# A conditioned two-layer feed-forward kernel: layer 1's adapters computed for four chunks in one go, in four PSUM banks

## The chip, the cores and the metric

The kernel runs on one core of one Trainium2 chip. The metric is the device time of one execution in microseconds (us), as the median of several runs; lower is better. Everything is float32. In the trace the engines are called PE (TensorE, the matrix engine; its weight loads are a row of their own, PEld), DVE (VectorE), ACT (ScalarE), POOL (GpSimd) and SP (SyncE, which here only issues DMAs).

## The reference, cut to what matters

The input `x` has 64 batches x 32 positions x 512 features, that is 2048 tokens. Layer 0 (a long convolution, then a linear layer with routed low-rank adapters) is added to `x`; layer 1 follows. The change touches only the first half of layer 1, a gated feed-forward block of width F = 1376 in which every batch has a low-rank adapter of rank 16 of its own:

```
def lora_add(base, inp, A, B):
    Ab = A[layer_idx][lora_indices]
    Bb = B[layer_idx][lora_indices]
    t = jnp.einsum('bri,bni->bnr', Ab, inp)
    return base + jnp.einsum('bor,bnr->bno', Bb, t) * SCALE
gate = lora_add(jnp.einsum('bnh,fh->bnf', x, W_gate), x, A_gate, B_gate)
up = lora_add(jnp.einsum('bnh,fh->bnf', x, W_up), x, A_up, B_up)
act = jax.nn.silu(gate) * up
down = lora_add(jnp.einsum('bnf,hf->bnh', act, W_down), act, A_down, B_down)
```

Its result goes to a mixture of 16 experts, whose router first computes `logits = x2 @ gate_w.T` of the layer's input and takes the two best experts for each token.

## The kernel before, in words

**Order of the work.** The instructions of PE, DVE and ACT run in exactly the order in which the Python code names them (`tc.manual_schedule` over these three engines); waits between engines are put in by the framework. So "earlier in the code" means earlier in that engine's queue, and an instruction that waits holds up all that stand behind it on its engine. The DMAs that SP and POOL issue are placed by the framework.

**Groups and chunks.** Layer 1's gated block works through 8 groups of 8 batches (`for g in range(NG)`), a group being 256 tokens, and in each group through 11 chunks of 128 of the 1376 (padded to 1408) hidden features (`for j in range(NF)`). In one chunk:

- PE forms gate and up of the chunk as seven products of half-size blocks (a Strassen-like scheme, `by_blocks`, L789): four of them into one PSUM bank `gu`, three into a second bank `gum` (`more` in the code). Both come from the pool `ps_mm`, which has two banks; they take turns, so `gu` of chunk j has the bank of `gu` of chunk j-1 as long as nothing else takes one.
- ACT copies `gu` to SBUF (L925). DVE adds the parts up (L928, L929, L930), adds the adapter's share (L931), and then adds what is in `gum` (L937, L938). L938 is the last reader of the bank `gum`.
- ACT takes the Silu (L940), DVE multiplies (L942), and PE multiplies the result by `W_down` one chunk later (`down`, L852), adding up in the four banks `zp` of the pool `ps_acc`.

**The adapters.** `adapted` (L791) computes the adapters' share of gate and up. The adapter of a group is a product over 64 rows, so two matmuls of 64 rows run side by side in the upper and lower half of PE's array (L802, `which` 0 and 1), each into its own bank. In the kernel before, it is called at every even j for two chunks, takes the two banks of the pool `ps_td`, and ACT copies both to the SBUF tile `los` (L807). I call the L802 matmuls of one call a **visit**: PE comes from the 128-row products, does a visit and goes back. There are six visits in a group, at j = 0, 2, 4, 6, 8 (two chunks) and 10 (one chunk). In the trace each matmul of this float32 code counts as two, so a visit for two chunks shows as x16.

**What else uses the same banks and queues.**

- At the end of a group: `ranks` (L825, the adapters' first factor for the next group; DVE copies it out in L835), the last `down`, then `own` (L866 to L876): DVE reads `zp` four times (L866), and ACT and DVE each copy two halves of it to `zt` (L876).
- In chunk j = 0 of the next group: `turn_own` (PE L880, ACT L882) between the two banks of the chunk, and `adapt` (PE L889, DVE L892) at its end; in j = 1 `turn` (PE L901, four transposes per bank, two banks of `ps_td`, copied out by DVE and ACT in L904).
- In groups 2, 4 and 6 the router's logits: at the end of j = 2 `logits` (PE L735, ACT L737), at the end of j = 3 `by_tokens` (PE L743 turns them, DVE L745 copies them out; one bank of `ps_td`), and in j = 4 and 5 `chosen` (softmax and the two best, about twenty small DVE operations and an Exp on ACT).
- At j = 6 `gathered_down` (four ACT copies, L454) for the next group's adapters, which POOL gathers by indirect DMA in j = 2 to 8 (L432); small DVE copies `columns` (L445) from j = 6 on. In group 0 DVE also forms sums of weights in each chunk up to j = 8 (`combine`, L209 to L212, four operations).

Of the kernel before, what the change touches and what calls it, by code (L numbers as in the profile page):

```python
# [9 lines left out]
F32 = mybir.dt.float32  # L10
I32 = mybir.dt.int32
AF = mybir.ActivationFunctionType
ALU = mybir.AluOpType
# [4 lines left out]
P = 128  # L18
# [8 lines left out]
F, NF = 1376, 11  # L27
# [10 lines left out]
NG, TG = B // GB, GB * H  # L38
# [4 lines left out]
FP = NF * P  # L43
# [60 lines left out]
def kernel(ctx: ExitStack, tc: tile.TileContext, a: dict, out: bass.AP):  # L104
    nc = tc.nc
    mm, tt, ts = nc.tensor.matmul, nc.vector.tensor_tensor, nc.vector.tensor_scalar
# [6 lines left out]
    ps_mm = ctx.enter_context(tc.tile_pool(name="ps_mm", bufs=2, space=PSUM))  # L113
    ps_td = ctx.enter_context(tc.tile_pool(name="ps_td", bufs=2, space=PSUM))
    ps_acc = ctx.enter_context(tc.tile_pool(name="ps_acc", bufs=4, space=PSUM))

    def bank(pool, name):
        return pool.tile([P, TB], F32, tag="bank", name=name)
# [5 lines left out]
    def rows(x, n):  # L124

        return x.unsqueeze(1).to_broadcast([x.shape[0], n, x.shape[1]])
# [47 lines left out]
    first = ExitStack()  # L174
# [18 lines left out]
    def fetch(n):  # L193

        g, j = divmod(n, NF)
        blocks[n] = stream.tile([P, 7 * BW], F32, tag="w", name=f"w_{n}")
        if g == 0:
            nc.sync.dma_start(blocks[n][:, 0 : 4 * BW], a["cw"][j])
        else:
            nc.sync.dma_start(blocks[n][:, 0 : 3 * BW], a["cw"][j][:, 0 : 3 * BW])  # L200
            nc.sync.dma_start(blocks[n][:, 3 * BW :], sums_d[j])
# [4 lines left out]
    def combine(n):  # L206

        a11, a12, a22, a21, s2, s3, s4 = (block(n, i) for i in range(7))
        tt(s3, a11, a21, ALU.subtract)  # L209
        tt(a21, a21, a22, ALU.add)  # L210
        tt(s2, a21, a11, ALU.subtract)
        tt(s4, a12, s2, ALU.subtract)  # L212
        (nc.gpsimd if n < 2 else nc.sync).dma_start(sums_d[n], blocks[n][:, 3 * BW :])
# [9 lines left out]
    def small(n=H):  # L223
        part = next(r for r in room if r[1] >= n)
        part[1] -= n
        return part[0][:, part[1] : part[1] + n]
# [46 lines left out]
    start = small(1)  # L273
# [187 lines left out]
    with tc.tile_pool(name="l0", bufs=1) as l0, tc.tile_pool(name="l0b", bufs=2) as l0b:  # L461
# [48 lines left out]
        def by_tokens(tb, yT):  # L510

            for i in range(4):
                n = tb * 4 + i
                gt = bank(ps_td, f"gt_{n}")
                for c in range(NC):
                    mm(
                        gt[:, 0 : G0 + P],
                        yT[:, c, i * P : (i + 1) * P],
                        ag[:, c, :],
                        start=(c == 0),  # L520
                        stop=(c == NC - 1),
                    )
                tt(hg[:, n, :], gt[:, 0:G0], row0[:, 0:G0], ALU.add)
                nc.scalar.copy(tmp[tb][:, i, :], gt[:, G0 : G0 + P])
# [261 lines left out]
    def by_blocks(to, n, i, x):  # L786

        for c in range(2):
            mm(to, block(n, i)[:, c * P : (c + 1) * P], x[:, c], start=(c == 0), stop=(c == 1))  # L789

    def adapted(g, j, r, wb):  # L791


        js = range(j, min(j + 2, NF))
        banks = [bank(ps_td, f"lo_{g}_{j}_{which}") for which in range(2)]
        for k, half in ((k, half) for k in js for half in (1, 0)):
            at = (k - j) * TG + (1 - half) * P
            lo = half * FP + k * P
            for which in range(2):
                mine = slice(which * P // 2, (which + 1) * P // 2)  # L800
                to = banks[which][:, at : at + P]
                mm(to, wb[mine, lo : lo + P], r[mine, half, :], start=True, stop=True)  # L802
        to = l1.tile([P, 2, 4, P], F32, tag="lo", name=f"los_{g}_{j}", bufs=1)
        n = len(js)
        for which in range(2):
            src = banks[which][:, 0 : n * TG].rearrange("p (j k t) -> p j k t", j=n, k=2)
            nc.scalar.copy(to[:, 0:n, 2 * which : 2 * which + 2], src)  # L807
        return to

    l1s = ExitStack()  # L810
    l1 = l1s.enter_context(tc.tile_pool(name="l1c", bufs=2))
# [8 lines left out]
    def ranks(g, wr):  # L820

        ps = bank(ps_td, f"r_{g}")
        for half in range(2):
            for c in range(NC):
                mm(  # L825
                    ps[:, half * P : (half + 1) * P],
                    wr[:, half, c, :],
                    batches(g, c, half),
                    start=(c == 0),
                    stop=(c == NC - 1),  # L830
                )
        r = l1.tile([P, 2, P], F32, tag="r", name=f"rs_{g}")
        own = cst[:, C_HALF : C_HALF + HG].unsqueeze(1).to_broadcast([P, 2 * H, HG])
        by_batch = ps[:, 0 : 2 * P].rearrange("p (n b) -> p n b", b=HG)
        tt(r.rearrange("p k (h b) -> p (k h) b", b=HG), by_batch, own, ALU.mult)  # L835
        return r
# [71 lines left out]
    r = ranks(0, wr)  # L908
    differ(0)
    past = None  # L910
    for g in range(NG):
        wa, wb, wd = got[g]
        this = Group(g)
        before = None
        for j in range(NF):
            n = g * NF + j
            (b11, b12, b21, b22), (t1, t2, t3, t4) = halves[g], differences[g]
            if j % 2 == 0:
                adapters = adapted(g, j, r, wb)
            ps = bank(ps_mm, f"gu_{g}_{j}")  # L920
            for at, i, x in ((0, 4, t2), (1, 0, b11), (2, 5, t3), (3, 2, t4)):
                by_blocks(ps[:, at * P : (at + 1) * P], n, i, x)
            gu = l1.tile([P, 4, P], F32, tag="gu", name=f"gus_{g}_{j}")
            flat = gu.rearrange("p k t -> p (k t)")
            nc.scalar.copy(flat, ps)  # L925
            if j == 0 and past is not None:
                past.turn_own()
            tt(gu[:, 0], gu[:, 0], gu[:, 1], ALU.add)  # L928
            tt(gu[:, 2], gu[:, 2], gu[:, 0], ALU.add)  # L929
            tt(gu[:, 3], gu[:, 3], gu[:, 2], ALU.add)  # L930
            tt(flat, flat, adapters[:, j % 2].rearrange("p k t -> p (k t)"), ALU.add)  # L931
            more = bank(ps_mm, f"gum_{g}_{j}")
            for at, i, x in ((0, 6, b22), (1, 1, b21), (2, 3, t1)):
                by_blocks(more[:, at * P : (at + 1) * P], n, i, x)
            if n + 4 < NG * NF:
                fetch(n + 4)
            tt(flat[:, 0:TG], flat[:, 0:TG], more[:, 0:TG], ALU.add)  # L937
            tt(gu[:, 0:3:2], gu[:, 0:3:2], rows(more[:, TG : TG + P], 2), ALU.add)  # L938
            si = glu.tile([P, TB], F32, tag="si", name=f"si_{g}_{j}")[:, 0:TG]
            nc.scalar.activation(si, flat[:, 0:TG], AF.Silu)  # L940
            at = glu.tile([P, TB], F32, tag="at", name=f"at_{g}_{j}")[:, 0:TG]
            tt(at, si, flat[:, TG:], ALU.mult)  # L942
            at = at.rearrange("p (k t) -> p k t", k=2)
            if g == 0 and j + 2 < NF:
                combine(j + 2)
            if g + 1 < NG and j == 9:
                differ(g + 1)
            if past is not None:
                if j == 0:
                    past.adapt()  # L950
                if j == 1:
                    past.turn()
                    columns(g, 9)
                if j == 2:
                    columns(g, 10)
            if g + 1 < NG and j >= 2:
                if j == 2:
                    coming.append(Adapters(g + 1))
                    got.append(coming[-1].all())
                coming[-1].rows(2 if j < 6 else 1)  # L960
            if before is not None:
                this.down(j - 1, before)
            before = at
            if g % 2 == 0 and g > 0:
                if j == 2:
                    lt = logits(g // 2 - 1)
                if j == 3:
                    by_tokens(g // 2 - 1, lt)
                if j == 4:
                    choice = chosen(g // 2 - 1)  # L970
                    next(choice)
                if j == 5:
                    run(choice)
            if g + 1 < NG and 6 <= j:
                if j == 6:
                    wr = gathered_down(g + 1)
                for i in ((0, 1), (2, 3), (4, 5), (6, 7), (8,))[j - 6]:
                    columns(g + 1, i)
        if g + 1 < NG:
            r = ranks(g + 1, wr)  # L980
            this.down(NF - 1, before)
            this.own()
        past = this


# [424 lines left out]
```

## Time and profile before

| | |
|---|---|
| median of 3 runs | 1040.71 us (1040.18 to 1041.33) |
| the profiled execution, its own time | 1042.03 us |
| its span, first to last instruction | 1040.2 us |
| PE busy | 1009.4 us (97%) |
| DVE, ACT, POOL busy | 563.7, 254.1, 168.4 us |
| granted TensorE clock | 1.000 of full speed over the whole span |
| the chunk loop of layer 1, first visit to last `down` of group 7 | 167.9 to 719.8 us |

In a timeline row the first number is the start in us from the beginning of the span, the second the time from the start of the first to the end of the last instruction of the merged row, then the engine, the line in the kernel, the operation, written tile <- read tiles, the shape, and the count; in brackets stands how long the engine sat idle before it and what released it. PE's matmuls overlap, so the time that a step takes is read from start to start, not from the durations. In a row of the waits stand: who waited, on which line, for whom; the total in us, how many times, and the longest.

### The profile page before, as it was taken

How to read it: one execution, taken by the hardware profiler on the slowest of the kernel's cores; microseconds unless marked ns; L12 is line 12 of the kernel's file. 1: busy time of each engine (PE TensorE's matmuls, PEld its weight loads, DVE VectorE, ACT ScalarE, POOL GpSimd, SP SyncE). 2: the span in 40 equal slices, each digit the busy share in tenths (PEclk: the TensorE clock that was granted, in tenths of full speed). 3: DMA queues.
4: the chain of work that ended last, by engine and by line, in shares of the span. 5: the costliest groups of instructions: out<-in, count | busy, mean ns of one | idle time of the engine just before them, and what ended most of it. 6: DMA issues, size and time to landing. Idle time of an engine off the chain costs nothing. (4 is left out here: it accounts for less than half of the span.)

```text
span 1040.2 us, 16572 instructions
## 1 busy us (share of the span) xinstructions
PE 1009.4 (97%) x6112; PEld 767.4 (74%) x6112; DVE 563.7 (54%) x1772; ACT 254.1 (24%) x509; POOL 168.4 (16%) x188
## 2 busy tenths in 40 slices
PE   3999999999999999999999999999999999999998
PEld 2777657888888888888888888897445677775453
DVE  5656566775464755656655556544632333332562
ACT  2222012222322332324223233232100222221000
POOL 2131001210201202102012021000000332221720
PEclk9999999999999999999999999999999999999999
DMA  6656409784755746646567457431930455555651
GB/s 179 203 210 225 134 20 344 242 286 147 237 180 185 243 155 205 232 160 210 184 197 248 147 194 242 147 123 38 418 132 11 121 163 164 169 168 178 203 183 60
DMA packets 63824, 189.42 MB, mean 182 GB/s; under 512 B 8448, under 2 KB 11552, under 8 KB 63104
## 3 DMA queue, kind: packets, MB, share of 16 engines
q1 hardware_dynamic: 49072, 137.52, 38.0%
q0 software_dynamic: 14096, 50.76, 16.3%
q8 instruction: 51, 0.84, 0.3%
q14 instruction: 29, 0.24, 0.1%
q10 hardware_dynamic: 576, 0.07, 0.1%
HBM read 157.56 MB, written 30.75 MB: 181 GB/s over the span
## 5 line engine op out<-in xcount | busy, mean ns | idle before, releaser
L852 PE MATMUL zp<-wn,at 128*128 128x288 f32 x704 | 185.4, 406 | 0.8 <-DVE at L942 0.8
L789 PE MATMUL gu<-t,w 128*128 128x128 f32 x1056 | 152.5, 281 | 0.0
L852 PEld LDWEIGHTS zp<-wn,at 128*128 128x128 f32 x704 | 127.1, 190 | 28.9 <-DVE at L942 0.9
L789 PEld LDWEIGHTS gu<-t,w 128*128 128x128 f32 x1056 | 133.9, 191 | 14.8 <-issue 5.9
L770 PE MATMUL sgu<-xall,sw 128*128 128x512 f32 (+2 forms) x272 | 114.1, 570 | 0.0
L432 POOL DMA_INDIRECT wa<-in_la,row_a x64 | 61.3, 958 | 309.8 <-issue 108.5
L928 DVE TENSOR_TENSOR gus<-gus 128x128 f32<-128x128 f32 x88 | 25.7, 292 | 134.6 <-ACT gus L925 134.6
L940 ACT ACTIVATE si<-gus 128x256 f32<-128x256 f32 x88 | 36.7, 417 | 244.7 <-DVE gus L938 244.7
L789 PE MATMUL gum<-xall,w 128*128 128x128 f32 x704 | 93.2, 275 | 0.8 <-DVE gus L938 0.7
L770 PEld LDWEIGHTS sgu<-xall,sw 128*128 128x128 f32 x272 | 49.7, 190 | 55.1 <-issue 53.5
L789 PEld LDWEIGHTS gum<-xall,w 128*128 128x128 f32 x704 | 85.7, 192 | 1.2 <-PE gu L789 1.1
L1186 POOL DMA_INDIRECT zr<-zd,tok x42 | 39.5, 941 | 255.3 <-DVE tok L1163 160.5
L1205 PE MATMUL egu<-wall,zx 128*128 x336 | 80.5, 382 | 0.0
L1205 PEld LDWEIGHTS egu<-wall,zx 128*128 128x128 f32 x336 | 60.5, 189 | 19.5 <-ACT zx L1196 12.5
L925 ACT COPY gus<-gu 128x512 f32<-128x512 f32 x88 | 51.4, 584 | 78.5 <-PE gu L789 78.5
L802 PEld LDWEIGHTS lo<-rs,wb 64*128 64x128 f32 x704 | 45.9, 187 | 26.2 <-issue 14.2
L802 PE MATMUL lo<-rs,wb 64*128 64x128 f32 x704 | 57.0, 287 | 5.8 <-ACT xall L904 2.5
L931 DVE TENSOR_TENSOR gus<-gus,los 128x512 f32<-128x512 f32 x88 | 60.9, 692 | 3.0
L942 DVE TENSOR_TENSOR at<-si,gus 128x256 f32<-128x256 f32 x88 | 37.4, 425 | 42.9 <-ACT si L940 42.9
L577 PE MATMUL main<-yT,w 128*128 128x512 f32 x128 | 58.4, 599 | 0.0
L807 ACT COPY los<-lo 128x512 f32<-128x512 f32 (+1 forms) x96 | 48.0, 551 | 42.4 <-PE lo L802 42.4
L1005 PE MATMUL op<-sat,sw 128*128 128x512 f32 x128 | 57.4, 594 | 0.3 <-PEq L1249 0.3
(275 smaller groups left out, 1306.3 us busy)
## 6 DMA issues: line engine op xcount, KB each, us to landing
w<-sums_d SPq DMA_DIRECT2D x77, 512.0 KB, 4.7
w<-in_cw SPq DMA_DIRECT2D x77, 384.0 KB, 3.7
wall<-in_xw SPq DMA_DIRECT2D x16, 768.0 KB, 15.1
yd<-eys SPq DMA_DIRECT2D x42, 256.0 KB, 2.8
g<-kpad SPq DMA_DIRECT2D x15, 512.0 KB, 5.6
w<-in_cw SPq DMA_DIRECT2D x11, 512.0 KB, 6.0
sums_d<-w SPq DMA_DIRECT2D x9, 512.0 KB, 3.4
xall<-in_xT SPq DMA_DIRECT2D x4, 1024.0 KB, 9.1
```

The lines of the kernel that those rows point to most:

```text
L432: nc.gpsimd.indirect_dma_start(to, None, src, at)
L577: mm(ps, w0[:, c, o * P : (o + 1) * P], yT[:, c, :], start=(c == 0), stop=(c == NC - 1),)
L770: mm(to, sw[j][:, i : i + P], mine, start=(c == 0), stop=(c == NC - 1))
L789: mm(to, block(n, i)[:, c * P : (c + 1) * P], x[:, c], start=(c == 0), stop=(c == 1))
L802: mm(to, wb[mine, lo : lo + P], r[mine, half, :], start=True, stop=True)
L807: nc.scalar.copy(to[:, 0:n, 2 * which : 2 * which + 2], src)
L852: mm(self.zp[half][s][:, 0 : DW - TW], at[:, 1 - half, :], wn[:, j, s, lo : lo + DW - TW], start=(j == 0), stop=(j == NF - 1),)
L925: nc.scalar.copy(flat, ps)
L931: tt(flat, flat, adapters[:, j % 2].rearrange("p k t -> p (k t)"), ALU.add)
L1005: mm(op[o], sw[j][:, i : i + P], at, start=(j == 0), stop=(j == NS1 - 1))
L1186: nc.gpsimd.indirect_dma_start(zr, None, zd[:, :], bass.IndirectOffsetOnAxis(ap=tok[:, t : t + 1], axis=0))
L1205: mm(ps[:, 0:256], x[:, c, :], wflat()[:, bass.ds(start + c * 256, 256)], start=(c == 0), stop=(c == NC - 1))
```

## The change

- `adapted` now does four chunks in one call, at j = 0, 4 and 8 (three chunks at 8, since there are eleven). It first does chunks j+2 and j+3 into the two banks of `ps_mm` (the banks of `gu` and `gum`) and emits ACT's two copies of them, then chunks j and j+1 into the two banks of `ps_td` with two copies. The SBUF tile `los` holds four chunks, twice the size. The number of matmuls and copies stays the same.
- `own` of the group that has ended no longer stands at its end but behind the first visit of the next group, so its two ACT copies come behind the visit's four.
- `by_tokens` no longer stands at the end of chunk 3 but between the two banks of chunk 3: PE turns the logits between `gu` and `gum`, and DVE copies them ahead of L928.

```
@@ def adapted(g, j, r, wb):
-        js = range(j, min(j + 2, NF))
-        banks = [bank(ps_td, f"lo_{g}_{j}_{which}") for which in range(2)]
-        for k, half in ((k, half) for k in js for half in (1, 0)):
-            at = (k - j) * TG + (1 - half) * P
-            lo = half * FP + k * P
+        to = l1.tile([P, 4, 4, P], F32, tag="lo", name=f"los_{g}_{j}", bufs=1)
+        for pool, first in ((ps_mm, j + 2), (ps_td, j)):
+            js = range(first, min(first + 2, NF))
+            n = len(js)
+            banks = [bank(pool, f"lo_{g}_{first}_{which}") for which in range(2)]
+            for k, half in ((k, half) for k in js for half in (1, 0)):
+                at = (k - first) * TG + (1 - half) * P
+                lo = half * FP + k * P
+                for which in range(2):
+                    mine = slice(which * P // 2, (which + 1) * P // 2)
+                    mm(banks[which][:, at : at + P], wb[mine, lo : lo + P], r[mine, half, :], start=True, stop=True)
             for which in range(2):
-                mine = slice(which * P // 2, (which + 1) * P // 2)
-                to = banks[which][:, at : at + P]
-                mm(to, wb[mine, lo : lo + P], r[mine, half, :], start=True, stop=True)
-        to = l1.tile([P, 2, 4, P], F32, tag="lo", name=f"los_{g}_{j}", bufs=1)
-        n = len(js)
-        for which in range(2):
-            src = banks[which][:, 0 : n * TG].rearrange("p (j k t) -> p j k t", j=n, k=2)
-            nc.scalar.copy(to[:, 0:n, 2 * which : 2 * which + 2], src)
+                src = banks[which][:, 0 : n * TG].rearrange("p (j k t) -> p j k t", j=n, k=2)
+                nc.scalar.copy(to[:, first - j : first - j + n, 2 * which : 2 * which + 2], src)
@@ the chunk loop
-            if j % 2 == 0:
+            if j % 4 == 0:
                 adapters = adapted(g, j, r, wb)
+            if j == 0 and past is not None:
+                past.own()
...
             if j == 0 and past is not None:
                 past.turn_own()
+            if j == 3 and g % 2 == 0 and g > 0:
+                by_tokens(g // 2 - 1, lt)
...
-            tt(flat, flat, adapters[:, j % 2].rearrange("p k t -> p (k t)"), ALU.add)
+            tt(flat, flat, adapters[:, j % 4].rearrange("p k t -> p (k t)"), ALU.add)
...
                 if j == 2:
                     lt = logits(g // 2 - 1)
-                if j == 3:
-                    by_tokens(g // 2 - 1, lt)
...
             this.down(NF - 1, before)
-            this.own()
         past = this
```

## The prediction

> **What bounds the kernel now.** I read the page's busy times first, then PE's waits, then PE's timeline in layer 1, then ACT and DVE beside it. Busy time and waits:
>
> ```profile
> PE 1009.4 (97%) x6112; PEld 767.4 (74%) x6112; DVE 563.7 (54%) x1772; ACT 254.1 (24%) x509; POOL 168.4 (16%) x188
> PE lo L802 <- ACT xall L904: 2.5, 7, 0.7
> PE lo L802 <- DVE lg L745: 2.0, 3, 0.7
> PE gum L789 <- DVE gus L938: 0.7, 2, 0.4
> ```
>
> PE is the bound: nearly everything counts that makes PE's queue longer or makes it stop. The waits put only 4.5 us on the adapters' bank pool. The rest of what a visit costs shows only in PE's timeline, from start to start (group 1; no visit, a two-chunk, a one-chunk visit, and the visit of chunk 2):
>
> ```profile
> 275.02 2.11 PE L852 MATMUL zp<-wn,at 128*128 128x288 f32 x8
> 276.97 0.61 PE L789 MATMUL gu<-t,w 128*128 128x128 f32 x4
> 277.41 0.61 PE L789 MATMUL gu<-xall,w 128*128 128x128 f32 x4
> ...
> 280.09 2.11 PE L852 MATMUL zp<-wn,at 128*128 128x288 f32 x8
> 282.13 1.16 PE L802 MATMUL lo<-rs,wb 64*128 64x128 f32 x16
> 283.22 0.71 PE L789 MATMUL gu<-t,w 128*128 128x128 f32 x4
> 283.77 0.61 PE L789 MATMUL gu<-xall,w 128*128 128x128 f32 x4
> ...
> 291.51 2.11 PE L852 MATMUL zp<-wn,at 128*128 128x288 f32 x8
> 293.55 0.71 PE L802 MATMUL lo<-rs,wb 64*128 64x128 f32 x8
> 294.19 0.71 PE L789 MATMUL gu<-t,w 128*128 128x128 f32 x4
> 294.74 0.61 PE L789 MATMUL gu<-xall,w 128*128 128x128 f32 x4
> ```
>
> From zp's start to the second gu row it is 2.39 us without a visit, 3.68 with two chunks, 3.23 with one. So a visit costs 1.29 or 0.84: 0.45 per chunk and 0.39 for going to 64 rows and back.
>
> The other view is ACT and DVE against PE, in an even group (the first two rows) and in group 0:
>
> ```profile
> 348.74 2.28 ACT L454 COPY wr<-wa 128x256 f32<-128x256 f32 x4
> 353.77 0.42 DVE L938 TENSOR_TENSOR gus<-gus,gum 128x256 f32<-128x256 f32 x1
> 210.85 1.20 ACT L454 COPY wr<-wa 128x256 f32<-128x256 f32 x2 [1.96 <-DMA wa<-in_la,row_a]
> ```
>
> L938 of chunk 7 ends at 354.19; PE begins the visit of chunk 8 at 352.59. Today this costs nothing, since a visit uses other banks. After the change the visit needs the bank that L938 reads.
>
> **What the change removes.**
>
> Per group: before 5 x 1.29 + 0.84 = 7.29 us of visits; after, two visits of four chunks (0.39 + 4 x 0.45 = 2.19) and one of three (1.74), 6.12. That is -1.17 in each of 8 groups. TensorEngine Tiling (Array Packing), section Key Properties, says that changing the tiling mode drains TensorE; it gives no price. If a drain cost nothing, this term would be 0; by the rows it is 0.39 for each of 24 visits less, -9.4, which I take.
>
> Chunk 2, groups 1 to 7: its visit waits for L904's banks. zp starts at 244.87, the second gu row at 249.50: 4.63, against 3.68. That 0.95 goes, x7 = -6.6.
>
> Chunk 4, groups 2, 4, 6: with L743 ahead and the wait for L745, zp at 326.45 to the second gu row at 331.39 is 4.94, 1.26 over 3.68. By_tokens in its new place costs what the like transpose L880 costs between gu and gum (gu x8 to gum is 1.00 at 305.27, else 0.89): 0.11. So -1.15, x3 = -3.5. What it waits for, ACT's L737, ends at 323.69, PE gets there at 325.0. DVE's L745 (0.22) would run at about 325.4, and the L928 behind it waits for ACT until 325.93 anyway; if that cover failed, 0.2.
>
> Gross: -19.5.
>
> **What it adds: waits for gum's bank at chunks 4 and 8.** Which = 1 of the new visit's first pair needs L938 of the chunk before, 0.05 after its end (L745 ends 329.70, lo goes on 329.75), and restarting costs 0.1 (14 matmuls took 1.09, where 16 take 1.09). Behind it in PE's queue stand the whole visit, gu and gum. A plain chunk is 5.07 long on PE; L938 ends 5.3 after its gu starts, 0.15 into a visit.
>
> - Chunk 4: odd groups and 7, 0.2 each (4); even ones 0.1 (3): 1.1.
> - Chunk 8, odd groups: the four L454 copies hold L925 of chunk 7 up by 0.8, L938 ends at 283.02, the visit's start is 282.13: 0.93, x3 = 2.8. Group 7 has no L454: 0.2.
> - Chunk 8, even groups: DVE's top-two work runs back to back from 342.40 to 345.82 and sets L928 of chunk 6. Today the visit of chunk 6 gives it 1.29 us; without it, counting from gu of chunk 4, gum of chunk 7 would start at 17.10 but its bank comes at 17.54 (+0.05): 0.49. L925 of chunk 7 still hangs on that chain: L938 ends at 23.35, the visit could start at 21.03: 2.37. With two restarts 3.05, x3 = 9.2.
> - Group 0: DVE has 5.35 per chunk (L928 at 198.42, combine's end at 203.77), more than PE's 5.07. The longer first visit (+0.90) shifts DVE's chain with it; L938 of chunk 3 ends 189.57 + 0.42 + 0.91 = 190.90, the visit could start at 189.05: 1.9. At chunk 8 L454 waits for the gathered rows; those land 2.9 (group 1) to 5.4 us (group 0) after issue, I take 4.2: L938 of chunk 7 ends at 216.4, visit possible at 213.4: 3.0 (2.2 to 4.2). Less the waits that vanish (0.4 at gum of chunk 9, and part of L942's 0.75), group 0 ends 2.4 later than now (1.6 to 3.7), its -1.17 counted in.
>
> By group, the savings counted in: group 0 +2.4; odd 1, 3, 5: -1.17 - 0.95 + 0.2 + 0.93 = -1.0, -3.0; even: -1.17 - 0.95 - 1.15 + 0.1 + 3.05 = -0.1, -0.3; group 7: -1.17 - 0.95 + 0.4 = -1.7. **Sum -2.6 to -3.0; I take -2.9.**
>
> TensorE: Matmul & The Clock Gate, section Part 1, says that an idle window of about 3.4 us halves the clock. The trace has a clock of 1.000 with gaps up to 0.75 us in this loop. My waits of 3.0 and less stay below; only group 0's upper end (4.2) would reach it, and then some 3.4 us at half speed would cost 1.7 more. I take 0.
>
> **Costed at nothing.** *The copies of the four banks:* counted from the visit's start S, the first copy starts at S + 1.25 (260.53 against 259.28), ends at S + 1.83; gu of chunk j, which needs that bank, comes at S + 2.0. Slack 0.13; the second copy (start + 0.49) serves gum, at S + 3.8. *own behind them:* ACT is done with four copies at S + 3.3; own's two (0.63 for such a pair) end at about S + 4.0, L925 is due at S + 4.1. Without that cover L925 slips by up to 0.7, and gum of chunk 1 has 1.0 in hand (L938 ends 309.63, gum starts 310.65). zp is next needed at chunk 1's end. DVE's order is untouched there. Nothing is issued or moved on SP or POOL. *The bigger tile:* DVE must have read the old one before ACT writes; that read precedes L938, which is waited for anyway.
>
> **The rivals.**
>
> 1. *As summed* (0.48): -2.9 on the profiled execution (1042.03, of which 1040.2 span; the median, 1040.71, is 1.3 lower): 1037.8, own range 1036 to 1038.6.
> 2. *The waits eat it all* (0.29): landing of 5.4 in group 0 (+1.3) and 0.1 to 0.2 more in each of 16 waiting visits (+1.6 to +3.2) leave 0 to +1.6: 1040.7, within 0.2%, which is about what a measurement of this kernel can tell from no change. For it: two thirds of the gain go in waits that I have from chains of ten operations. Against: the rows repeat to 0.02 between groups 1, 3 and 5.
> 3. *The bank copies bound the visit* (0.18, slower): the same tiling page, section PSUM Bottleneck, warns that tiling speeds up TensorE but not the emptying of PSUM. Place: gu of chunks 0, 4, 8 in `ps_mm`. By the rule all four copies would count (up to 1.3 a visit); by the row there is 0.13 slack. It turns the sum once the first copy ends 0.25 later than I have it (0.12 x 24 = 2.9). If gu had to wait for the second copy too (+0.49, so 0.36 late), 24 x 0.36 = 8.6: 1046.4. For it: four copies in a row where two stood. Against: gu and the first copy share the bank, not the second.
> 4. *The waits don't arise* (0.05): if the pool gave banks so that DVE's lateness stayed hidden, most of the 19.5 remains: about 1026.
>
> **The numbers.** Likeliest 1037.8. Range 1034.5 to 1043: case 1 and 2 with their bounds and the near part of 3. Faster by over 0.2%: 0.53 (cases 1 and 4); within: 0.29; slower: 0.18.
>
> **What would show it.** L802 in 24 visits, three to a group, x32, x32 and x24, with 2.0 us from a visit's start to gu when nothing waits. No waits of L802 for L904 or L745; in their place PE waiting for DVE L938 at L802 (chunks 4, 8), some 16 times, about 15 us in all, and three times at gum. No wait of gu for L807: if that appears, case 3. Group 0 longer, group 7 shorter by 1.7. Wrong would be the sum if the waits at chunk 8 of the even groups are not near 2.4 us, since those three weigh most.

## The result, and the profile after

The changed kernel took 1047.09 us in the median (1045.56 to 1048.15, 4 runs), the kernel before 1040.45 beside it: a ratio of 1.0061, interval 1.0044 to 1.0079. It is 0.6% slower, where I had forecast 0.3% faster and a range that ended at 1043. (The lines of the loop have moved: the visit's matmul is L805 now, gum's last reader L943, ACT's copy of `gu` L928, the Silu L945, the bank copies L808; the experiments below shift them by a few more.)

Busy times and PE's waits for gum's bank after, to be laid beside those of before:

```profile
span 1044.6 us, 16552 instructions
PE 1005.8 (96%) x6112; PEld 774.1 (74%) x6112; DVE 564.0 (54%) x1772; ACT 253.3 (24%) x509; POOL 169.0 (16%) x188
PE lo L805 <- DVE gus L943: 12.8, 8, 2.3
PE gum L789 <- DVE gus L943: 1.6, 4, 0.4
```

The waits for L904 and L745 are gone, as the prediction said, and in their place stands the wait for gum's bank, 12.8 us. No wait of `gu` for a bank copy (L808) appears. Most of what I had not forecast is in no wait at all. The granted TensorE clock was 1.000 over the whole span before; now it is 0.993, and in the four runs 0.993 to 0.995. The timeline of group 0 at the visit of chunk 8 shows where:

```profile
212.46 0.48 PE L805 MATMUL lo<-rs,wb 64*128 64x128 f32 x2
214.64 0.42 DVE L943 TENSOR_TENSOR gus<-gus,gum 128x256 f32<-128x256 f32 x1
215.20 2.90 PE L805 MATMUL lo<-rs,wb 64*128 64x128 f32 x22 [2.26 <-DVE gus L943]
218.03 1.22 PE L789 MATMUL gu<-t,w 128*128 128x128 f32 x4
219.04 1.06 PE L789 MATMUL gu<-xall,w 128*128 128x128 f32 x4
```

The visit's first pair goes, the second waits for L943 to end at 215.06. Then the other 22 matmuls take 2.83 us to the start of gu; in group 7, which does not wait, a whole visit of 24 takes 1.80. The gu rows behind are slow too: 1.01 from the first to the second, 0.55 elsewhere. The view by stretches says why. I put the ends of the stretches where the clock changes, and in group 2 at the same spacing; the columns are the stretch, its length, PE's busy time and count, the granted clock, the DMA share and GB/s (group 0, then groups 4, 6 and 2):

```profile
211.58:214.99 3.41, 1.36 (x6) 1.00 0.97 294
214.99:218.40 3.41, 3.20 (x23) 0.50 0.82 323
218.40:221.82 3.42, 3.42 (x18) 0.50 0.87 285
221.82:225.23 3.41, 3.41 (x23) 1.00 0.41 144
...
491.47:494.89 3.42, 1.54 (x9) 1.00 0.89 285
494.89:498.30 3.41, 3.41 (x25) 0.50 0.67 237
498.30:501.71 3.41, 3.41 (x30) 1.00 0.44 173
...
631.42:634.83 3.41, 1.53 (x12) 1.00 0.92 315
634.83:638.24 3.41, 3.41 (x27) 0.50 0.62 221
638.24:641.65 3.41, 3.41 (x28) 1.00 0.36 145
...
351.53:354.94 3.41, 3.10 (x17) 1.00 0.47 120
354.94:358.35 3.41, 1.85 (x25) 1.00 0.89 357
```

The clock is at half for 6.83 us in group 0 and for 3.41 in groups 4 and 6. The three falls lie 279.90 and 139.94 us apart, which is 82 and 41 times 3.413: the clock changes on a grid of 3.41 us. In the stretch ahead of each fall PE was busy for only 1.36 to 1.54 us; no other stretch of the loop had less than 1.85, and none of those was followed by a fall.

So it matters where on the grid a stop lies. PE stops equally long in group 2 (the first row) and in group 4, and in group 2 the clock stays:

```profile
356.50 1.57 PE L805 MATMUL lo<-rs,wb 64*128 64x128 f32 x22 [1.88 <-DVE gus L943]
494.87 2.89 PE L805 MATMUL lo<-rs,wb 64*128 64x128 f32 x22 [1.88 <-DVE gus L943]
```

In group 4 the whole stop, 492.99 to 494.87, lies in one stretch. In group 2 it runs from 354.62 to 356.50, and an edge at 354.94 divides it, so that 1.85 us of work are left in the poorer of the two stretches.

The length of each group, from its first visit's start to the next group's, before, after, and in four of the experiments below:

| group | 0 | 1 | 2 | 3 | 4 | 5 | 6 |
|---|---|---|---|---|---|---|---|
| before | 67.29 | 67.99 | 70.47 | 68.00 | 70.47 | 68.37 | 70.46 |
| after | 72.52 | 67.44 | 70.26 | 68.11 | 71.85 | 67.75 | 72.09 |
| e2_fill | 69.50 | 67.35 | 70.27 | 68.19 | 70.28 | 67.46 | 70.50 |
| e4_gather7 | 68.42 | 66.38 | 68.51 | 67.04 | 68.52 | 66.59 | 68.76 |
| e7_four_once | 67.00 | 66.65 | 67.97 | 66.65 | 67.96 | 66.65 | 67.97 |
| e9_best | 65.48 | 66.37 | 67.97 | 66.78 | 67.97 | 66.41 | 67.97 |

After against before, groups 0, 4 and 6, where the clock fell, are longer by 5.23, 1.38 and 1.63; the other four together are 1.3 shorter. Group 7 up to the router's counting is 1.6 shorter (85.95 against 87.56).

### The profile page after: what moved, and what is told of

It is laid out like the page before. It is cut to its first block, busy times and chain, and to the rows that moved or that the text cites. A ratio compares the mean times of both kernels' runs of the same rounds, so it can differ in the third digit from the quotient of the medians.

```text
span 1044.6 us, 16552 instructions
## 1 busy us (share of the span) xinstructions
PE 1005.8 (96%) x6112; PEld 774.1 (74%) x6112; DVE 564.0 (54%) x1772; ACT 253.3 (24%) x509; POOL 169.0 (16%) x188
## 5 line engine op out<-in xcount | busy, mean ns | idle before, releaser
L789 PEld LDWEIGHTS gu<-t,w 128*128 128x128 f32 x1056 | 137.9, 194 | 14.7 <-issue 6.6
L945 ACT ACTIVATE si<-gus 128x256 f32<-128x256 f32 x88 | 36.7, 417 | 251.5 <-DVE gus L943 251.5
L928 ACT COPY gus<-gu 128x512 f32<-128x512 f32 x88 | 51.5, 585 | 87.8 <-PE gu L789 87.8
L805 PE MATMUL lo<-rs,wb 64*128 64x128 f32 x704 | 54.6, 293 | 13.4 <-DVE gus L943 12.8
L805 PEld LDWEIGHTS lo<-rs,wb 64*128 64x128 f32 x704 | 48.4, 199 | 23.7 <-issue 22.6
L808 ACT COPY los<-lo 128x512 f32<-128x512 f32 (+1 forms) x96 | 46.9, 560 | 49.6 <-PE lo L805 49.5
```

The lines of the kernel that those rows point to most:

```text
L805: mm(banks[which][:, at : at + P], wb[mine, lo : lo + P], r[mine, half, :], start=True, stop=True)
L808: nc.scalar.copy(to[:, first - j : first - j + n, 2 * which : 2 * which + 2], src)
```

## The experiments

Theory A: the loss sits at the visit of chunk 8. It waits for the bank that L943 of chunk 7 reads, and the longest of these waits (A1) let the clock fall. Rivals: the four-bank visit itself costs (four copies in a row, `own` and `by_tokens` moved), or the slow rows come from restarting after a wait and not from a clock that reacts to the idling.

**e1_split8:** chunk 8 and 10 get their old visits in `ps_td` back.

```
-        for pool, first in ((ps_mm, j + 2), (ps_td, j)):
+        for pool, first in ((ps_mm, j + 2), (ps_td, j))[0 if j < 8 else 1 :]:
-            if j % 4 == 0:
+            if j in (0, 4, 8, 10):
+                base = j
```

(and `adapters[:, j - base]` for `j % 4`; so in all kernels that mix the two kinds of visit.)

> The changed kernel, but the visits of chunks 8 and 10 as they were before (two chunks and one chunk, in the banks of ps_td); four chunks at a time only at chunks 0 and 4. Theory A: the loss sits in the visit of chunk 8, which waits for the bank that L938/L943 of chunk 7 reads last (2.5 us in group 0, 0.9 to 1.5 in odd groups, 2.2 in even ones), and the long ones of these waits are followed by a clock at half for about 2 us. Then the split costs 8 x 0.39 = +3 and removes waits and clock loss: about -16 against the changed kernel, so 1030 to 1033 us, clock 1.000. Rival B: the loss is in the four-bank visit itself (four copies in a row, own and by_tokens moved), wherever it stands: then two of three such visits in a group remain, and no more than a third of it goes, 1043 us or more. Rival C: gains of fewer visits are smaller than 0.39 each: then between the two, near 1037.

Measured 1029.69 us, ratio to before 0.9894 (0.9877 to 0.9910), clock 1.000, just below the 1030 to 1033 expected. That is 17.4 us less than the changed kernel, with eight visits more. Two four-bank visits in each group are left, and they cost little. Its waits for gum's bank:

```profile
PE lo L805 <- DVE gus L944: 1.3, 1, 1.3
PE gum L789 <- DVE gus L944: 2.0, 5, 0.4
```

The one long wait left for a visit is group 0's at chunk 4. Rivals B and C fall.

**e2_fill:** the changed kernel, with work for PE in the wait.

```
+            if j == 8 and g % 2 == 0:
+                idle = bank(ps_td, f"idle_{g}")
+                for _ in range(10 if g == 0 else 8):
+                    mm(idle[:, 0:P], ident, block(n, 0)[:, 0:P], start=True, stop=True)
             if j % 4 == 0:
```

> The changed kernel with 8 unread matmuls of 128 columns (10 in group 0) put on PE ahead of the visit of chunk 8 in groups 0, 2, 4, 6; their results are not used. They take 0.22 us each, 1.8 us (2.2 in group 0), that is less than PE waits there (2.2 and 2.5 us). Theory A1 (the wait lets the clock fall): PE isn't idle any more, the clock stays at 1.000, the visit of chunk 8 and the gu behind it run at full speed, and 5 to 6 us go: 1041 to 1042 us, although PE has 7.6 us more work. Rival A2 (the slow rows after the wait come from restarting, not from a clock that reacts to idling): the same rows stay slow, 1047 us or more.

Measured 1041.17 us (1040.22 to 1044.65, 12 runs), 1.0008 of before (0.9998 to 1.0017). So 5.9 us went although PE has some 7.6 us more to do. The timeline in group 4:

```profile
489.78 1.95 PE L922 MATMUL idle<-w,cst 128*128 128x128 f32 x16
491.65 2.16 PE L805 MATMUL lo<-rs,wb 64*128 64x128 f32 x24
493.74 0.71 PE L789 MATMUL gu<-t,w 128*128 128x128 f32 x4
494.29 0.61 PE L789 MATMUL gu<-xall,w 128*128 128x128 f32 x4
```

The unread matmuls take 1.87 from start to start, the visit behind them 2.09 instead of 5.18 from its first pair, and gu's rows are back at 0.55. The rows were slow because of the clock, and the clock because PE stood still: A1 holds. Four of its 12 runs still came out at 0.996 to 0.998 of the clock, and those took 1042.35 to 1044.65. In the profiled one the clock stayed at 1.000, and group 3, which was not filled, still waits 1.62 us at chunk 8.

**e10_fill_half:** half of that work, 4 matmuls in groups 2, 4, 6 and 5 in group 0.

> e2_fill with half the unread matmuls: 4 before the visit of chunk 8 in groups 2, 4, 6 and 5 in group 0 (0.9 and 1.1 us). PE still waits there, 1.3 us instead of 2.2, in group 0 about 1.4. Theory A1 (a wait of about 2 us lets the clock fall, in some executions one of 1.6 us, none of about 1.3): clock 1.000, 1041 us as e2_fill, since the unread work lies in the waits. Rival (any stop of PE there lets the clock fall, or the unread matmuls themselves had kept it up by their number): clock near 0.997, 1043 to 1045 us.

Measured 1041.59 us (1040.32 to 1043.78, 12 runs), 1.0009 (1.0000 to 1.0018). PE's visits wait 9.1 us in all now and 4.6 in e2_fill, and the time is the same: what the filling bought was the clock. The waits were 0.99 in groups 2, 4, 6 (1.3 expected), 1.34 in group 0 and, unfilled, 1.89 in group 3, all at full clock in the profiled execution. Again four of 12 runs had 0.998. Group 3's stop is as long as those that halved the clock before, but it too is divided by an edge of the grid, at 421.76 (this execution's clock record runs from 22.40 to 1039.57, 298 times 3.413):

```profile
418.34:421.76 3.42, 2.30 (x10) 1.00 0.87 281
421.76:425.17 3.41, 2.64 (x32) 1.00 0.50 200
```

**e3_tokens:** the kernel before, with `by_tokens` alone moved between the banks of chunk 3.

> The kernel before with by_tokens alone moved between the two banks of chunk 3 (groups 2, 4, 6); visits of two chunks in ps_td as before. By the sum of the prediction -1.15 us for each of three groups: 1037.0 us, no wait of L802 for L745. Rival: PE only waits for DVE elsewhere instead: 1040.4.

Measured 1037.08 us, 0.9968 (0.9956 to 0.9981). Groups 2, 4 and 6 are 69.32, 69.32 and 69.31 long, 1.15 less than before each, as the sum had it; this part of the change is good by itself. (Group 0, which has no `by_tokens`, came out 0.68 shorter in the profiled execution; that is not explained.)

**e4_gather7:** the changed kernel, with what makes L943 late taken away: the four ACT copies of `gathered_down` (L454) stand behind L928 of chunk 7, in the time in which ACT waits for DVE.

```
             nc.scalar.copy(flat, ps)
+            if g + 1 < NG and j == 7:
+                wr = gathered_down(g + 1)
...
-                if j == 6:
-                    wr = gathered_down(g + 1)
```

> The changed kernel with the four ACT copies of gathered_down (L454) put behind L925/L928 of chunk 7, where ACT has 2.7 us idle, and no longer at the end of chunk 6, ahead of it. Theory A (L454, late by itself or waiting for gathered rows, holds L925 of chunk 7 up, so L938/L943 comes late, so the visit of chunk 8 waits): waits at chunk 8 fall to 0.2 us in groups 1, 3, 5, to about 0.9 in 2, 4, 6, in group 0 to about 1.7 (there DVE's own copies L445 wait for the same rows); the clock stays up except perhaps in group 0: 1033 to 1037 us. Rival: DVE's chain alone sets L938/L943: waits at chunk 8 stay as they are, 1046 us or more.

Measured 1031.05 us, 0.9908 (0.9891 to 0.9925), clock 1.000: 16 us less than the changed kernel, with all three four-bank visits kept, and below the 1033 to 1037 expected. Group 4 in the changed kernel, and in this one:

```profile
489.27 2.29 ACT L454 COPY wr<-wa 128x256 f32<-128x256 f32 x4
491.46 0.57 ACT L928 COPY gus<-gu 128x512 f32<-128x512 f32 x1
494.30 0.42 DVE L943 TENSOR_TENSOR gus<-gus,gum 128x256 f32<-128x256 f32 x1
```

```profile
481.07 0.57 ACT L928 COPY gus<-gu 128x512 f32<-128x512 f32 x1
481.54 2.31 ACT L454 COPY wr<-wa 128x256 f32<-128x256 f32 x4
484.31 2.17 PE L805 MATMUL lo<-rs,wb 64*128 64x128 f32 x24
484.35 0.42 DVE L945 TENSOR_TENSOR gus<-gus,gum 128x256 f32<-128x256 f32 x1
```

With L454 ahead, L928 starts 2.19 after it; with L454 behind, gum's last reader ends 0.46 after the visit's start, and the visit takes 2.11. The waits for gum's bank at visits fall from 12.8 to 3.0 us. The rival, that DVE's chain alone sets L943, falls.

**e8_before_gather7:** a control, that move alone in the kernel before.

> A control: the kernel before with nothing but the four copies L454 moved behind L925 of chunk 7. Theory A (a late L938 costs nothing while visits use other banks): 1040.5 us, no change, perhaps 0.5 less in group 0. Rival (those copies cost PE time on their own, whatever the banks): as much as e4_gather7 gained without the clock, 4 to 8 us less, 1033 to 1036.

Measured 1039.91 us (20 runs), 0.9989 (0.9982 to 0.9996). Only group 0 is shorter (65.62 against 67.29); all others are the same to 0.01. So outside group 0 a late L938 was harmless while the visits had other banks; it is the change that put a price on it.

**e5_split_g0:** e4_gather7 with group 0 back at two chunks a visit from chunk 4 on.

> e4_gather7 with group 0 alone back to visits of two chunks at chunks 4, 6, 8 and 10 in ps_td (its first visit keeps four). In e4_gather7 group 0 still waits 1.3 us at chunk 4 and 1.2 at chunk 8, and takes 68.4 us. Theory A (each wait for gum's bank is paid in full unless DVE bounds the group anyway): group 0 falls to about 67, the whole to 1029.7 us. Rival: group 0 is bound by DVE's 5.35 us per chunk, then nothing goes and the two added visits cost up to 0.8: 1031 to 1032.

Measured 1027.47 us, 0.9870 (0.9853 to 0.9886). Group 0 went from 68.42 to 65.39, twice what I expected: it was not bound by DVE's 5.35 us a chunk. From start to start its two waits had cost 1.79 and 1.41 (3.78 and 3.21 to gu, against 1.99 and 1.80 without a wait); less 0.8 for the two added visits that is 2.4, and the last 0.6 is not assigned.

**e6_own_back:** e4_gather7 with `own` at the end of its group again.

> e4_gather7 with own back at the end of its group, ahead of the next group's first visit. Theory A (own's place costs and brings nothing, its two ACT copies are done before ACT could begin with the visit's): 1031 us as e4_gather7, within 0.7. Rival: own's copies hold up the four bank copies, gu of chunk 0 waits for its bank in groups 1 to 7, up to 0.5 us each: 1034.5.

Measured 1030.28 us, 0.9898 (0.9881 to 0.9914), against 0.9908 with it moved; group lengths agree within 0.1. The move of `own` brings nothing that can be measured.

**e7_four_once:** four chunks only at chunk 0, else two.

> Four chunks at a time only at chunk 0, where no wait arises; visits of two chunks in ps_td at 4, 6, 8 and one chunk at 10; by_tokens and own where the change put them. Against e1_split8 this has one visit more in each group (8 x 0.39 = +3.1) and no waits at chunk 4 (about -1.3 in group 0 and 0.1 to 0.25 in the others, together -2.5). Theory A: 1030.3 us, within 1 of e1_split8. Rival (fewer visits bring less than 0.39 each, the gain of e1_split8 came from elsewhere): 1028 or less. If e1_split8's gain came from the second four-bank visit: 1033 or more.

Measured 1027.62 us, 0.9874 (0.9857 to 0.9890): 2.1 less than e1_split8, outside the 1 us I gave it, and where I had put the rival. The steps, read from start to start, decide against the rival all the same. From zp to the second gu row it is 4.57 with a four-chunk visit that does not wait, against 2.39 without a visit and 3.68 with two chunks: 2.18 against twice 1.29, so a visit less saves 0.40. The odd groups are 0.13 longer than in e1_split8 (66.65 against 66.52): 0.40 for the added visit less 0.25 for the wait at chunk 4 (2.24 there to gu, 1.99 at chunk 0). The even ones are 0.38 shorter (67.97 against 68.35): 0.40 for the visit, less 0.09 for the wait at chunk 4, less 0.69 at chunk 7, where gum waited for its bank in e1_split8 (2.40 from gu to gum against 1.78 here, and gum 1.41 against 1.34). I had left this last term out; the visit of chunk 6 lets DVE catch up. Group 0 is 1.2 shorter.

**e9_best:** for each kind of group the shortest arrangement so far: even groups four chunks at chunk 0 and then two, odd ones four throughout, L454 behind L928 of chunk 7.

```
-        for pool, first in ((ps_mm, j + 2), (ps_td, j)):
+        for pool, first in ((ps_mm, j + 2), (ps_td, j))[0 if j == 0 or g % 2 == 1 else 1 :]:
-            if j % 4 == 0:
+            if j % 4 == 0 or (g % 2 == 0 and j in (6, 10)):
+                base = j
```

> Each group takes the arrangement that was shortest for its kind in the runs so far, with L454 behind L925 of chunk 7: even groups as in e7_four_once (four chunks at chunk 0, then two at a time in ps_td; 68.0 us where e5_split_g0 has 68.5), odd ones as in e5_split_g0 (four at 0, 4 and 8; 66.4), group 0 as in e5_split_g0 (65.4). Theory A (the groups' lengths add): three even groups 0.5 shorter than in e5_split_g0, 1027.5 - 1.6 = 1025.9 us. Rival (the groups pull on each other): 1027.5.

Measured 1025.48 us, 0.9852 (0.9835 to 0.9868), clock 1.000: better than both kernels by 1.5% and 2.1%, and near the 1025.9 that adding the groups' lengths gave. What PE still waits for at gum's bank:

```profile
PE gum L789 <- DVE gus L946: 0.3, 1, 0.3
PE lo L805 <- DVE gus L946: 0.2, 1, 0.2
```

## Why the prediction was wrong, point by point

- **The gross gain** held. Visits went from 48 to 24 and a four-chunk visit takes 1.99 to gu where nothing waits (predicted 2.0); e3_tokens shows the 1.15 at chunk 4; L904's waits are gone. A visit less saves 0.40 by the steps under e7_four_once (predicted 0.39).
- **The waits for gum's bank** were forecast at the right places and nearly the right sizes. From the first pair's start to L943's end: chunk 8 in group 0 2.6 (3.0 forecast), in even groups 2.2 (2.37), chunk 4 in group 0 1.7 (1.9); chunk 7's gum waits 0.43 (0.49). The small ones at chunk 4 of the other groups show as visits of 2.08 to 2.25 instead of 1.99.
- **The step that failed: "My waits of 3.0 and less stay below [...] I take 0."** I had read the idle window of about 3.4 us that the Trainium skill gives (TensorE: Matmul & The Clock Gate, section Part 1) as a bar that a shorter stop does not reach. Here a stretch of 3.41 us with 1.36 to 1.54 us of work in it was enough, and stops with 1.88 to 2.26 us of idle time made three of those: 6.83 + 3.41 + 3.41 us at half speed, worth about 6.8 us of PE's work. e2_fill measured 5.9 us. I even gave the mechanism a price (1.7), but for one group and for an end of the range that did not come.
- **A term mis-sized: chunk 8 in odd groups,** 0.93 each. I allowed for late gathered rows in group 0 only. In the changed kernel ACT waits for them in groups 1, 3 and 5 too, by 0.21, 0.88 and 0.52. It gets there earlier (in group 3 its first copy starts 40.9 us into the group, 42.4 before), which fits the missing visit of chunk 6. Group 3:

```profile
420.09 1.20 ACT L454 COPY wr<-wa 128x256 f32<-128x256 f32 x2 [0.88 <-DMA wa<-in_la,row_a]
```

  The time from the first pair to L943's end at chunk 8 became 1.2, 1.9 and 1.5 us in groups 1, 3 and 5. With the clock held up (e2_fill) these groups came out at -0.64, +0.19 and -0.91 against before, where I had -1.0 each: 1.6 us in sum.
- **Adding up:** -2.9 forecast, +5.9 for the clock, +1.6 for the gathered rows gives +4.6. In the two profiled executions the loop (groups 0 to 6, and 7 up to the router's counting) is 5.4 longer. Between the medians it is +6.6; the last 2 us are not assigned, and the changed kernel's four runs lie 2.6 apart.
- **Costed at nothing, and rightly:** `own` (e6_own_back) and the four bank copies. The slower rival named the right sign for the wrong reason, since no gu waits for a copy. The mechanism for "slower" should have been the clock behind the waits that I had just computed.

The bound is known only as far as these runs show it. In the loop of the changed kernel a stretch with 1.54 us of work was followed by a fall and one with 1.85 was not. The twelve profiled executions, each on its own grid, have no exception; nearest are the ends of two, where PE runs out of work: 1.29 us (e8_before_gather7) and the clock fell, 1.57 (e7_four_once) and it held. Left open is why group 0 stayed at half for two stretches. In the first of them PE was busy for 3.20 us, in groups 4 and 6 for all 3.41; that this is the reason is not shown.

## What to carry to other kernels

Giving PE other banks saves nothing if the reader of those banks is later than the bank's next use: for each bank that a step takes, find the last reader's end beside the moment PE needs it, in every kind of iteration, and look for what holds the reader up (here four copies on ACT, cheap to move). A stop of PE of two microseconds must be priced with the clock behind it, though whether it is paid depends on how the stop lies on the clock's grid; unread matmuls in the stop are a cheap test of that. And take the parts apart: `by_tokens`' move alone gave 0.3%, and the four-chunk visit was worth having only where the bank was free.

## What the runs showed of the hardware that I had not expected

The TensorE clock fell to 0.50 after stops of PE well shorter than 3.4 us (1.88 to 2.26 by the idle time in the rows), and came back after 3.41 or 6.83 us. What decided was PE's work in one stretch of a grid of 3.41 us. That the clock is judged in windows of 3.4 us that run on whatever the kernel does is what the Trainium skill states (TensorE: Matmul & The Clock Gate, section Part 1), and the falls, 82 and 41 times 3.413 us apart, agree with it. Its table has the clock fall after an idle window; in this trace the window need not be idle, since 1.36 to 1.54 us of work in it did not keep the clock up.

The grid lies differently from execution to execution: counted from the span's start, an edge is at 421.76 in the profiled e10_fill_half and at 423.21 in the changed kernel. So the same kernel can come out differently. Of the 24 executions of the two filled kernels eight had a mean clock of 0.996 to 0.998. As an estimate, 3.41 less the stop, group 3's stop would leave 1.52 us of work in e10_fill_half if it lay in one stretch, and 1.79 in e2_fill; e10's four would fit, e2's four would need a longer stop. That this is what happened is not shown, since the profiled execution of each is one at full clock.
